# Layer 3 of a four-layer convolution and attention kernel: ScalarE copies the second head pair's scores, VectorE masks the copies in place

## The chip, the cores and the metric

The kernel runs on one core of a Trainium2 chip. The metric is the device time of one execution in microseconds (us). Before the change three runs took 3665.39, 3681.4 and 3687.82 us; the median is 3681.4.

## The reference, cut to what matters

The input x is 4 images of 256 channels, 48 by 48, in fp32. Four layers follow each other, each of the form x = x + layer(group norm(x)): a 7x7 dilated attention kernel, two 3x3 convolutions, and, as layer 3, windowed linear attention. Only layer 3 is changed:

```python
q = sigmoid(Wq x); k = sigmoid(Wk x); v = (Wv x) / |v|      # 8 heads of 32 channels
Ik  = _integral(k)                     # running sums over rows and columns
Ikv = _integral(k[f] * v[g])
for w in (1, 2, 4):
    ws = 48 // w                       # window 48, 24 or 12, around each pixel
    attn = q . box(Ikv, ws);  norm = q . box(Ik, ws)
    outs.append(attn / (norm + 1e-6))
out = Wout @ concat(outs) + bout
```

For each pixel and each of three window sizes, a head sums k v over the keys in the window around the pixel, and multiplies by q. Swapping the order gives what the kernel computes: scores q . k of all pairs of a pixel and a key that are near enough, times a 0/1 mask (is the key in the pixel's window?), times v.

## The kernel before, in words

**Layer 3's tiles.** An image has 6 row blocks of 8 rows (`RB`). A block of queries is one row block of one image and one half of the channels (4 heads): 4 x 2 x 6 = 48 blocks (`order`). Keys are cut into tiles (a, c) of 8 rows and 16 columns, 128 keys, one a partition: row block a, column block c of 3. A block rb visits the key tiles up to three row blocks away (`tiles_of`, line 1913), 12, 15 or 18 of them, 720 in all. `HALVES` (line 78) are the half windows 24, 12 and 6, numbered wi = 0 (widest), 1 (middle), 2 (narrow). So there are three kinds of tile:

- near tiles, |a - rb| at most 1 (384 of them): all three windows see them (`many`, line 1831);
- tiles two rows away (192): the widest and the middle window;
- tiles three rows away (144): the widest window alone, and no row of queries sees them whole.

For near tiles and those two rows away the widest window holds a middle part of the columns whole (`rows_whole`, line 1739); that part comes from summed states and one set of matmuls a block (`whole`, line 1878). Only the outer columns are worked out from scores, in one strip of 16 columns (c = 0 or 2) or two of 8 (c = 1) (`strips`, line 1747). The order of tiles takes near tiles and others by turns, c = 1, 0, 2, and what near tiles are left over come last.

**One tile.** The loop at line 2077 hands out the work; the helper `InOrder` (line 135) keeps each engine's instructions in the order in which the program names them, and through it every instruction has line 143 in the profile.

1. TensorE: `scores` (line 1763) is called for two pairs of heads. A pair's scores, `s`, take one tile of two PSUM banks; the pool `ps_s` (line 1490) has two such tiles. So the first pair of the next tile needs the banks of this tile's first pair, and the second the second's. A matmul shows as two records; a tile has eight.
2. `masked` (line 1781) makes the masked scores `sm` in SBUF, in one tile a pair (pool `smp`, line 1488, 6 tiles: three tiles' worth). VectorE multiplies scores in PSUM by a mask in SBUF (`of_banks`, line 1825). In tiles two rows away ScalarE copies the middle part instead, unmasked (`copy`, line 1837).
3. GpSimd then multiplies (loop at line 1861), from SBUF to SBUF: in near tiles it makes the narrow window's part from the middle one's, and two rows away it masks ScalarE's copy in place.
4. TensorE: `sums` (line 1890) multiplies the masked scores by v into three accumulators `acc`, two tiles later (`LAG` = 2, line 83). TensorE's queue so reads: scores of tile n, sums of tile n - 2, scores of tile n + 1. At a window's last tile ScalarE copies the accumulator to `stage`.

In a near tile the middle part has 624 elements a partition (c = 1), 448 (c = 0) or 432 (c = 2) for a pair of heads; the strips have 256 (two times 128 with c = 1). Three rows away there are 560 to 768.

**The order within a tile** is written out by hand at lines 1854 to 1860 (`copy` does something two rows away alone, `middle` in near tiles alone):

```python
first, second = zip(ss, pairs)
copy(*second)
middle(*first)
widest(*first)
copy(*first)
middle(*second)
widest(*second)
```

After each tile `advance` (line 237) lets other jobs place a few instructions each: projections of the next image, key sums (`k_sums`, line 1535: VectorE scans `cs` and differences `pt`, GpSimd sums `pt`), norms (`norms`, line 1577: `nhi`, `nlo` on GpSimd), states of the keys (`state`, line 1672), and the end of a block (`prepare`, line 1927, `finish`, line 1960: `o`, `stage`, `out_ps`). They share the engines' queues with the tiles. SP issues the loads.

Of the kernel before, what the change touches and what calls it, by code (L numbers as in the profile page):

```python
# [146 lines left out]
def conv_preact_kernel(  # L147
# [53 lines left out]
    pe, dve, act, pool, sync = (  # L201
        InOrder(tc, e) for e in (nc.tensor, nc.vector, nc.scalar, nc.gpsimd, nc.sync)
    )
# [249 lines left out]
    with (  # L453
# [479 lines left out]
        def load_row(pool_, tag, a):  # L933

            t = pool_.tile([P, NCT, K0, P], F32, tag=tag, name="wrow")
            sync.dma_start(
                out=t, in_=w1[:, a * K0 : (a + 1) * K0, :].rearrange("(ct p) k o -> p ct k o", p=P)
            )
            return t
# [442 lines left out]
        with tc.tile_pool(name="wst", bufs=1) as wst:  # L1382
            for ct in range(NCT):
                fetch_x(0, ct)
            rows = [load_row(k1p, "k1", 0), load_row(vp, "v", MT), load_row(vp, "v", MT - 1)]
# [43 lines left out]
        with (  # L1429
# [11 lines left out]
            first = ExitStack()  # L1441
# [41 lines left out]
    with (  # L1483
# [243 lines left out]
        def rows_seen(wi, a, rb):  # L1727

            h = HALVES[wi]
            return (  # L1730
                max(0, a * RB - h + 1 - rb * RB),
                min(RB, a * RB + RB + h - rb * RB),
            )

        def cols_seen(wi, c):
            h = HALVES[wi]
            return max(0, c * KC - h + (wi > 0)), min(W, c * KC + KC + h)

        def rows_whole(a, rb):

            return abs(a - rb) * RB + RB <= HALVES[0]
# [5 lines left out]
        def strips(c):  # L1747

            (c0, c1), (f0, f1) = cols_seen(0, c), cols_whole(c)
            return [(p0, p1) for p0, p1 in ((c0, f0), (f1, c1)) if p0 < p1]  # L1750

        class Block:
# [28 lines left out]
            def masked(self, a, c, ss):  # L1781

                rb = self.rb
                all0 = rows_seen(0, a, rb), cols_seen(0, c)
                (r0, r1), (c0, c1) = all0
                wis = [wi for wi in range(NW) if seen(wi, a, rb)]
                full = rows_whole(a, rb)
                pieces = {wi: [cols_seen(wi, c)] for wi in wis}
                if full:
                    pieces[0] = strips(c)  # L1790

                def room():

                    t = smp.tile([P, SM_ROOM], F32, tag="sm", name="sm")
                    at, got = 0, {}
                    for wi in wis:
                        nr = rows_seen(wi, a, rb)[1] - rows_seen(wi, a, rb)[0]
                        for p0, p1 in pieces[wi]:
                            n = 2 * nr * (p1 - p0)
                            got[wi, p0] = t[:, at : at + n].rearrange(  # L1800
                                "p (j r w) -> p j r w", j=2, r=nr
                            )
                            at += n
                    assert at <= SM_ROOM
                    return got

                pairs = [room() for _ in ss]

                def view(tiles, wi, rows, cols):
                    y0, _ = rows_seen(wi, a, rb)  # L1810
                    x0 = next(p0 for p0, p1 in pieces[wi] if p0 <= cols[0] and cols[1] <= p1)
                    return tiles[wi, x0][
                        :, :, rows[0] - y0 : rows[1] - y0, cols[0] - x0 : cols[1] - x0
                    ]

                def times_mask(engine, wi, rows, cols, dst, src):
                    mr = rb * RB + rows[0] - (a * RB - HALVES[wi] + 1)
                    mc = cols[0] - (c * KC - MCOL0[wi])
                    nr, ncol = rows[1] - rows[0], cols[1] - cols[0]
                    m = mask[wi][:, mr : mr + nr, mc : mc + ncol]  # L1820
                    engine.tensor_mul(
                        dst, src, m.unsqueeze(1).to_broadcast([P, 2, nr, ncol])
                    )

                def of_banks(s, tiles, wi, rows, cols):
                    src = s[:, :, rows[0] - r0 : rows[1] - r0, cols[0] - c0 : cols[1] - c0]
                    times_mask(dve, wi, rows, cols, view(tiles, wi, rows, cols), src)

                many = seen(NW - 1, a, rb)

                def middle(s, tiles):
                    if full and many:
                        of_banks(s, tiles, 1, rows_seen(1, a, rb), cols_seen(1, c))

                def copy(s, tiles):
                    if full and not many and 1 in wis:
                        rows, cols = rows_seen(1, a, rb), cols_seen(1, c)
                        act.copy(  # L1840
                            view(tiles, 1, rows, cols),
                            s[:, :, rows[0] - r0 : rows[1] - r0, cols[0] - c0 : cols[1] - c0],
                        )

                def widest(s, tiles):
                    if not full:
                        of_banks(s, tiles, 0, *all0)
                        return
                    for cols in pieces[0]:
                        of_banks(s, tiles, 0, (r0, r1), cols)  # L1850

                first, second = zip(ss, pairs)
                copy(*second)
                middle(*first)
                widest(*first)
                copy(*first)
                middle(*second)
                widest(*second)  # L1860
                for tiles in pairs:

                    wi = NW - 1 if many else 1
                    if wi in wis:
                        rows, cols = rows_seen(wi, a, rb), cols_seen(wi, c)
                        src = view(tiles, 1, rows, cols)
                        times_mask(pool, wi, rows, cols, view(tiles, wi, rows, cols), src)
                return pairs
# [40 lines left out]
        def seen(wi, a, rb):  # L1909
            r0, r1 = rows_seen(wi, a, rb)  # L1910
            return r0 < r1
# [165 lines left out]
        for n in range(len(stream) + LAG):  # L2077
            if n < len(stream):
                i, a, c, at, last = stream[n]
# [6 lines left out]
            if n >= LAG:  # L2086
                i, a, c, at, last = stream[n - LAG]
# [60 lines left out]
```

## Time and profile before

| what | value |
|---|---|
| median of three runs | 3681.4 us |
| the profiled execution | 3665.04 us |
| its span | 3663.2 us |
| granted TensorE clock, mean | 0.952 |
| busy over the span: TensorE, VectorE, ScalarE, GpSimd | 3216.3, 2419.0, 677.5, 1661.6 us |
| first and last product of masked scores on VectorE | begin at 1389.7 and 3631.9 us |
| products of masked scores on VectorE (`sm<-s,masks`) | 2592, 1145.8 us |
| score matmul records (`s<-qs,ks`) | 5760, 870.4 us |
| sums (`acc<-sm,vs`) | 14976, 683.0 us |
| masks on GpSimd (`sm<-sm,masks`) | 1152, 822.9 us |
| ScalarE's copies of scores (`sm<-s`) | 384, 123.4 us |

A line of groups names line, engine, operation, what is written and read, shape (partitions x elements, or rows * columns of the array for TensorE) and count; then the busy time and the mean of one in ns; then the idle time just before, and which instruction ended it. A line of the timeline begins with start and length in us of a row of like instructions that follow closely. A line of waits names who waited for whom: us in total, times, longest. A matmul's end is modelled in the profile, and spans on GpSimd are rough.

### The profile page before, as it was taken

To read this page: it belongs to the slowest core of one execution; us is meant where nothing else is said; L and a number is where in the kernel's file an instruction comes from. 1 tells how busy PE (TensorE), PEld (TensorE's weight loads), DVE (VectorE), ACT (ScalarE), POOL (GpSimd) and SP (SyncE) were. 2 spreads that over 40 slices of the span, in tenths; PEclk is the share of its full clock that TensorE was granted. 3 is DMA by queue.
4 is the path that set the end of the run, shared out by engine and by line. 5 is a ranking of instruction groups with operands and counts; after the bars stand their busy time and mean duration, and the time that the engine had idled before them with its cause. 6 is when DMAs were issued, how large, how long until landed. Compare 5 with 4: busy or idle time off the path is not lost. (4 is left out here: it accounts for less than half of the span.)

```text
span 3663.2 us, 73044 instructions
## 1 busy us (share of the span) xinstructions
PE 3216.3 (88%) x28754; PEld 1942.3 (53%) x28754; DVE 2419.0 (66%) x4987; ACT 677.5 (18%) x1557; POOL 1661.6 (45%) x2548
## 2 busy tenths in 40 slices
PE   3689998998997887887899889899998899999998
PEld 2467686786785664443444444444444444444444
DVE  7976587487484365876756576765577656566664
ACT  0012111111114422222101222211222201111100
POOL 0000120030030034787876786776476777454552
PEclk9789999999998898999999999999999999999999
DMA  7746324324314423344533543344223344211222
GB/s 252 227 139 197 105 94 129 112 85 127 102 65 138 136 72 108 122 141 144 149 103 112 157 122 122 108 126 137 81 96 120 119 128 129 64 32 32 66 62 61
DMA packets 373031, 423.29 MB, mean 116 GB/s; under 512 B 129075, under 2 KB 328531, under 8 KB 371539
## 3 DMA queue, kind: packets, MB, share of 16 engines
q1 hardware_dynamic: 371491, 416.32, 36.9%
q8 instruction: 229, 3.75, 0.4%
q0 software_dynamic: 144, 1.52, 0.2%
q14 instruction: 111, 0.91, 0.1%
q10 hardware_dynamic: 1056, 0.79, 0.1%
HBM read 288.79 MB, written 131.25 MB: 115 GB/s over the span
## 5 line engine op out<-in xcount | busy, mean ns | idle before, releaser
L143 DVE TENSOR_TENSOR sm<-s,masks 128x128 f32<-128x128 f32 (+8 forms) x2592 | 1145.8, 496 | 709.7 <-PE s L143 377.7
L143 POOL TENSOR_TENSOR sm<-sm,masks 128x432 f32<-128x432 f32 (+14 forms) x1152 | 822.9, 728 | 711.3 <-DVE sm L143 512.6
L143 PE MATMUL s<-qs,ks 32*128 32x320 f32 (+3 forms) x5760 | 870.4, 505 | 109.4 <-DVE sm L143 72.5
L143 PE MATMUL acc<-sm,vs 128*32 128x64 f32 (+13 forms) x14976 | 683.0, 308 | 32.2 <-POOL sm L143 32.1
L143 PE MATMUL cv<-vx,wt 128*128 128x288 f32 x2080 | 556.9, 423 | 92.3 <-DVE vx L143 49.5
L143 PEld LDWEIGHTS s<-qs,ks 32*128 32x128 f32 x5760 | 353.1, 188 | 479.8 <-issue 195.8
L143 PEld LDWEIGHTS acc<-sm,vs 128*32 128x32 f32 x14976 | 351.0, 111 | 441.6 <-issue 269.4
L143 PEld LDWEIGHTS cv<-vx,wt 128*128 128x128 f32 x2080 | 400.5, 197 | 212.6 <-issue 55.0
L143 POOL MEMSET v<- 128x16 f32 (+1 forms) x120 | 18.6, 215 | 722.4 <-DVE vx L143 628.3
L143 ACT COPY sm<-s 128x234 f32<-128x234 f32 (+5 forms) x384 | 123.4, 343 | 915.8 <-PE s L143 784.4
L143 PE MATMUL cv<-v,wl 128*128 128x384 f32 x1152 | 224.3, 354 | 22.4 <-DVE x L143 8.6
L143 PEld LDWEIGHTS cv<-v,wl 128*128 128x128 f32 x1152 | 214.6, 195 | 32.2 <-issue 15.2
L143 POOL TENSOR_TENSOR pt<-pt 128x144 f32<-128x144 f32 x336 | 185.3, 552 | 23.4 <-DVE pt L143 0.5
L143 POOL TENSOR_TENSOR v<-l2v,v 128x384 fp32r<-128x384 f32 x96 | 109.0, 1165 | 127.4 <-ACT v L143 118.7
L143 POOL TENSOR_TENSOR nhi<-nhi,nq 128x384 f32<-128x384 f32 x144 | 144.9, 1034 | 0.3
L143 PE MATMUL cv<-pad,wl 128*128 128x384 bf16 x864 | 143.1, 327 | 0.0
L143 PE MATMUL out_ps<-o,wout_sb 128*128 128x384 f32 x288 | 124.2, 514 | 12.3 <-DMA rc<-r_d 7.6
L143 ACT COPY stage<-acc 128x384 f32<-128x384 f32 x144 | 64.0, 489 | 303.7 <-PE acc L143 272.7
L143 PE MATMUL out_ps<-stage,wout_sb 128*128 128x384 f32 x288 | 118.4, 493 | 0.7 <-DVE stage L143 0.7
L143 DVE TENSOR_TENSOR vx<-v 128x868 f32<-128x868 f32 x112 | 115.3, 1055 | 0.5
L143 PEld LDWEIGHTS <-wl 128*128 128x128 bf16 x864 | 83.9, 97 | 59.4 <-issue 0.8
L143 DVE SCALAR_TENSOR_TENSOR x<-cv,alpha,x 128x384 f32<-128x384 f32 x144 | 83.9, 610 | 41.7 <-PE cv L143 41.4
(174 smaller groups left out, 3347.4 us busy)
## 6 DMA issues: line engine op xcount, KB each, us to landing
wt<-wt SPq DMA_DIRECT2D x48, 768.0 KB
kb_d<-pt SPq DMA_DIRECT2D x48, 576.0 KB
rc<-r_d SPq DMA_DIRECT2D x192, 144.0 KB
nhi<-kb_d SPq DMA_DIRECT2D x120, 192.0 KB
nlo<-kb_d SPq DMA_DIRECT2D x88, 192.0 KB
o_d<-stage SPq DMA_DIRECT2D x24, 576.0 KB
o<-o_d SPq DMA_DIRECT2D x24, 576.0 KB
wl<-wl_d SPq DMA_DIRECT2D x16, 768.0 KB
```

The lines of the kernel that those rows point to most:

```text
L143: return lambda *args, **kwargs: self.tc.keep_in_program_order(op(*args, **kwargs))
```

## The change

The three helpers are replaced by three others: `copy` (ScalarE copies a window's part of a pair), `cut` (VectorE masks a window's strips from PSUM, as `of_banks` did), and `again` (VectorE multiplies a part in SBUF by its mask, in place). For each kind of tile the order is now written out. In near tiles ScalarE copies the second pair's middle part; VectorE masks the first pair's strips and middle part and the second pair's strips from PSUM, and then the copy in place. Three rows away ScalarE copies the second pair whole, and VectorE masks the copy in place after the first pair. Two rows away the calls come in the order in which they came before.

```diff
-                def middle(s, tiles):
-                    if full and many:
-                        of_banks(s, tiles, 1, rows_seen(1, a, rb), cols_seen(1, c))
...
+                def copy(s, tiles, wi):
+                    rows, cols = rows_seen(wi, a, rb), cols_seen(wi, c)
+                    act.copy(
+                        view(tiles, wi, rows, cols),
+                        s[:, :, rows[0] - r0 : rows[1] - r0, cols[0] - c0 : cols[1] - c0],
+                    )
+
+                def cut(s, tiles, wi):
+                    for cols in pieces[wi]:
+                        of_banks(s, tiles, wi, rows_seen(wi, a, rb), cols)
+
+                def again(tiles, wi):
+                    rows, cols = rows_seen(wi, a, rb), cols_seen(wi, c)
+                    t = view(tiles, wi, rows, cols)
+                    times_mask(dve, wi, rows, cols, t, t)
...
                 first, second = zip(ss, pairs)
-                copy(*second)
-                middle(*first)
-                widest(*first)
-                copy(*first)
-                middle(*second)
-                widest(*second)
+                if not full:
+                    copy(*second, 0)
+                    cut(*first, 0)
+                    again(second[1], 0)
+                elif many:
+                    copy(*second, 1)
+                    cut(*first, 0)
+                    cut(*first, 1)
+                    cut(*second, 0)
+                    again(second[1], 1)
+                else:
+                    if 1 in wis:
+                        copy(*second, 1)
+                    cut(*first, 0)
+                    if 1 in wis:
+                        copy(*first, 1)
+                    cut(*second, 0)
```

More of the change, by code (lines that the diff above doesn't have):

```diff
@@ L1831, in masked @@
                 many = seen(NW - 1, a, rb)
-                def middle(s, tiles):
-                    if full and many:
-                        of_banks(s, tiles, 1, rows_seen(1, a, rb), cols_seen(1, c))
[L1837 to L1850, printed above, removed]
-                first, second = zip(ss, pairs)
-                copy(*second)
-                middle(*first)
-                widest(*first)
-                copy(*first)
-                middle(*second)
-                widest(*second)
+                def copy(s, tiles, wi):
[4 more added lines that the diff above has]
+                    )
```

## The prediction

> **What bounds it now.** I read, in this order: the page, the groups by shape for 2200 to 3600 us, the waits, the timeline. The tiles of layer 3 run from 1389 to 3640 us; nothing outside can change. There TensorE is busy 2042 of 2251 us, VectorE 1491, GpSimd 1504, ScalarE 401, by the window sums:
>
> ```profile
> core 0: us, PE busy (x) PEld busy (x) DVE busy (x) ACT busy (x) POOL busy (x), PEclk, DMA share, GB/s
> 1389.00:3640.00 2251.00, 2041.83 (x22896) 1016.62 (x22888) 1490.62 (x3180) 400.87 (x1044) 1503.60 (x2243) 0.97 0.36 106
> ```
>
> A busy TensorE isn't a full one. In the timeline of 3313 to 3323.5 us each row of `s` is one tile's eight score records, two pairs of heads:
>
> ```profile
> 3313.20 1.56 PE L143 MATMUL s<-qs,ks 32*128 32x384 f32 x8
> 3314.16 2.94 DVE L143 TENSOR_TENSOR sm<-s,masks 128x624 f32<-128x624 f32 x8 [0.37 <-PE s L143]
> ...
> 3315.59 1.94 PE L143 MATMUL s<-qs,ks 32*128 32x384 f32 x8
> 3316.58 0.33 PEld L143 LDWEIGHTS s<-qs,ks 32*128 32x128 f32 x4 [0.70 <-PE s L143]
> ...
> 3317.61 0.74 ACT L143 COPY sm<-s 128x312 f32<-128x312 f32 x2 [1.38 <-POOL sm L143]
> 3318.06 0.49 DVE L143 TENSOR_TENSOR sm<-s,masks 128x128 f32<-128x128 f32 x2 [0.96 <-ACT sm L143]
> ...
> 3321.12 0.91 PE L143 MATMUL s<-qs,ks 32*128 32x320 f32 x8
> ```
>
> Both pairs together take 0.91 us; where the second pair must wait until VectorE has left its banks they take 1.56 to 1.94, and count as busy. Sorting the score records by tile: a group takes 0.77 us (320 columns) or 0.88 (384) undisturbed. The excess over this, with the idle time before it, is 136 us behind near tiles with c=1 and a far tile next, 76 behind c=2, 23 behind c=0, 32 between near tiles, 64 behind tiles three rows away, 50 behind two: 381 us. That is the stake: the two score buffers make TensorE and VectorE take turns. The waits show only a part:
>
> ```profile
> PE s L143 <- DVE sm L143: 72.5, 205, 2.7
> PE acc L143 <- POOL sm L143: 32.1, 39, 5.2
> ```
>
> **The skill.** The Trainium skill, PSUM — Partial Sum Buffer, "PSUM bank collisions raise a hardware error": two engines must not be in one bank at once. So strips of the second pair follow ScalarE's copy: ACT ends at 3318.35 in the rows above for both copies, the second pair's at 3318.03, and DVE starts at 3318.06. SBUF — State Buffer, "Who interferes with whom": a VectorE instruction with two SBUF inputs and a GpSimd one that reads SBUF exclude each other, and the first keeps the port to its end. The trace agrees; VectorE's `stage` product has both inputs in SBUF:
>
> ```profile
> 2519.25 0.55 DVE L143 TENSOR_TENSOR stage<-stage,rc 128x384 f32<-128x384 f32 x1
> 2519.45 1.32 POOL L143 TENSOR_TENSOR sm<-sm,masks 128x216 f32<-128x216 f32 x2 [1.42 <-ACT sm L143]
> ...
> 2522.45 0.78 POOL L143 TENSOR_TENSOR sm<-sm,masks 128x324 f32<-128x324 f32 x1 [0.33 <-DVE sm L143]
> 2522.69 0.96 DVE L143 TENSOR_TENSOR stage<-stage,rc 128x384 f32<-128x384 f32 x1
> ```
>
> Ahead of GpSimd it takes 0.55 us. Behind it, it waits until GpSimd ends (2523.23) and then takes 0.42 more: its own time less 0.14. The products of today read `s` from PSUM and don't meet this.
>
> **The change, part by part.** Durations (means of the groups by shape):
>
> ```profile
> L143 DVE TENSOR_TENSOR sm<-s,masks 128x256 f32<-128x256 f32 x505 | 208.5, 416 | 94.5 <-POOL sm L143 34.7 <-issue 23.8 <-ACT sm L143 16.4
> L143 DVE TENSOR_TENSOR sm<-s,masks 128x624 f32<-128x624 f32 x170 | 136.2, 801 | 101.4 <-PE s L143 85.7 <-POOL sm L143 10.0 <-POOL nhi L143 2.3
> L143 DVE TENSOR_TENSOR sm<-s,masks 128x448 f32<-128x448 f32 x168 | 104.0, 619 | 80.5 <-PE s L143 34.9 <-issue 25.5 <-POOL sm L143 8.8
> L143 POOL TENSOR_TENSOR sm<-sm,masks 128x324 f32<-128x324 f32 x52 | 42.8, 834 | 6.1 <-DVE sm L143 5.9
> L143 ACT COPY sm<-s 128x312 f32<-128x312 f32 x42 | 16.3, 421 | 187.8 <-PE s L143 175.0 <-DVE pt L143 4.0 <-POOL pt L143 4.0
> ```
>
> (1) Removed: 384 middle products from PSUM and 144 whole ones. Added: as many in place, equally long alone: 384 elements with both inputs in SBUF took 0.55 us above, as the line through 0.416 (256) and 0.619 (448) from PSUM gives (0.551). So nothing, as long as GpSimd is out of the way; (4) prices it where it isn't.
>
> (2) Added: 528 ScalarE copies. From 168 elements (298 ns) to 312 (421), 0.85 ns an element over 0.155: 0.54 us for 448, 0.69 for 624, 0.52 for 432, 0.70 to 0.81 for 640 to 768; 384 × 0.58 + 144 × 0.75 = 331 us on an engine busy 401 of 2251. The second pair's scores are there about 0.1 us after VectorE begins a tile (median), so a copy ends at 0.75 to 0.95, before VectorE has done the first pair (0.95 to 1.2): free, except behind `stage`, `state` and sigmoid work on ScalarE's queue. Without that cover it would cost up to its length. I put 15 us, range 0 to 60.
>
> (3) The second pair's banks come free earlier. Near c=1: after two strips, the middle and two strips: 0.48 + 0.72 + 0.40 = 1.60 us, not 2.31; c=0: 1.38, not 1.82; c=2: 1.36, not 1.78. Three rows away: after a copy, about 1.0 to 1.3 us, not 1.5 to 1.8.
>
> (4) The in-place product meets GpSimd. GpSimd starts the first pair's narrow mask 0.15 us after the first middle: 1.35 to 2.2 in c=1. The in-place product, issued at 1.52, waits until 2.2 and takes 0.66: end 2.84 against 2.31. Likewise c=0 2.4 against 1.82, c=2 2.25 against 1.78: about +0.53 × 384 = 203 us of VectorE time, bounded by 0 (GpSimd idle) and +0.95 (behind a 1 us GpSimd job). Three rows away: +0.12 × 144 = 17. VectorE becomes 1491 + 220 = 1711. Behind it on VectorE's queue stand the next tile's first strips: late by that where its scores are already there. Against today's pace that is seldom: VectorE's gap to the next tile is under 0.55 us behind 123 of 384 near tiles, shortfall 34 us in all.
>
> (5) Walking the two queues. Rules from the trace: VectorE has scores 0.91 us (320) or 1.02 (384) after their matmul starts; a release reaches TensorE in 0.15; a second pair alone takes 0.74 or 0.85; sums take 1.25, 1.1, 1.0 us (near c=1, 0, 2), 0.84 to 0.7 (three rows), 0.7 to 0.6 (two). Before, near c=1 starting at 0: scores of the far tile at 1.35 and, second pair, 2.46; sums from 3.31 to 4.06; VectorE ends the far tile at 4.42; next near tile's scores at 4.06 and 4.57, VectorE at 4.97. After: 1.4 and 1.85, sums 2.3 to 3.05, but VectorE is held until 2.76 and releases the far tile's first pair at 3.72; next near scores at 3.87, VectorE at 4.78. Over three pairs (c=1, 0, 2) VectorE starts again after 13.85 before and 13.07 after with tiles three rows away; after 14.4 and 13.1 with tiles two rows away, which ScalarE already copies. There are 48 and 64 such triples, and 48 near tiles without partner (nothing): −(48 × 0.78 + 64 × 1.3) = −121 us. With each block's other work spread evenly (TensorE 0.83, VectorE 0.48 us a tile) a triple still gains 0.7.
>
> (6) What is late next: the second pair's narrow mask on GpSimd waits for the in-place product and ends about 1 us later. `acc` needs it two tiles on: the median slack is over 2.3 us, but moving all near tiles by 1.0 makes 44 late, 36 us.
>
> (7) No DMA, weight load or buffer is added; loads issued by SP keep their places. Two rows away the calls and their order are as before.
>
> Sum: −121 + 36 + 15 = −70. The profiled execution, 3665 us (span 3663), becomes 3595. It lies at the bottom of the runs shown; their median is 16 higher, so I forecast 3611.
>
> **Rivals.** *Given back (0.22).* GpSimd is 86% busy at 1550 to 1850 us; a near tile and one two rows away give it four masks (mean 728 ns on the page, 2.9 us), and its other jobs are (1504 − 823)/720 tiles, 1.9 us for two: 4.8 of the 6.2 us that two tiles take now. If it becomes the bound through the first half, half of −121 goes: −60 + 36 + 15 = −9, 3672. Against: it is half idle after 3200. *The port lock paces VectorE (0.28), slower.* If the in-place product of near tiles takes over 1.5 us on average, not about 1.2, a triple is back at 13.9 to 14.2 and the gain of (5) is gone; then 36 + 15 remain, and a tenth of VectorE's other 344 us, now in the way, 34: +85, 3766. For: GpSimd is busy two thirds of the time, with jobs of 1 us. Against: it decides only from 1.5 us. *The turns vanish wholly (inside the 0.50 of faster):* two thirds of 271 us (the 381 less the idle before scores and the two-row tiles) kept: about −130 net, 3550. That the second pair's banks aren't freed earlier is hardly possible: nothing reads them after the strips.
>
> **Numbers.** Faster 0.50 (likeliest, 3611; its own range 3535 to 3645), within 1% 0.22, slower 0.28; a measurement of this kernel can tell about 1% from no change. The range 3535 to 3750 leaves out the ends of both.
>
> **What would show it.** ScalarE near 730 us in these windows, VectorE near 1710; the mean in-place product of near tiles 1.05 to 1.3 us; score groups behind near c=1 tiles under 1.2 us, not 1.8; `acc` behind GpSimd some 35 us longer. It is wrong if the in-place product averages over 1.5 us, if strips wait for ScalarE in most near tiles, or if `acc` waits for GpSimd grow past 100 us.

## The result, and the profile after

The changed kernel takes 3716.3 us (median of 4 runs, 3715.5 to 3718.5) against 3679.5 us before (median of 4): ratio 1.0105, 95% interval 1.0073 to 1.0137. It is slower by about 37 us; 3611 was forecast. Its profiled execution has a span of 3713.7 us, 50 longer; layer 3's tiles take 2296 us, before 2250. In the lines below PE is TensorE, DVE VectorE, ACT ScalarE and POOL GpSimd.

The window sums, by image: first two together, third, fourth. Columns: stretch, its length, busy time (and instructions) of TensorE, of its weight loads, VectorE, ScalarE, GpSimd, then the granted clock, and share and GB/s of DMA. Before:

```profile
1388.00:2588.00 1200.00, 1066.80 (x11588) 525.86 (x11587) 808.73 (x1693) 231.67 (x589) 884.14 (x1304) 0.95 0.42 126
2588.00:3151.00 563.00, 515.79 (x5773) 257.24 (x5772) 374.60 (x810) 112.69 (x282) 375.86 (x566) 0.98 0.37 111
3151.00:3640.00 489.00, 460.25 (x5538) 234.07 (x5537) 307.86 (x680) 56.72 (x174) 243.61 (x373) 0.99 0.18 52
```

After:

```profile
1393.00:2648.00 1255.00, 1031.38 (x11592) 517.25 (x11596) 873.17 (x1693) 382.09 (x853) 960.35 (x1304) 0.93 0.40 120
2648.00:3226.00 578.00, 496.31 (x5776) 251.40 (x5771) 404.93 (x810) 188.32 (x414) 411.69 (x566) 0.96 0.36 109
3226.00:3690.00 464.00, 416.09 (x5538) 218.90 (x5537) 343.92 (x680) 136.80 (x306) 256.95 (x373) 0.99 0.18 53
```

This is the first thing to see: the change loses 55 and 15 us in the first three images and gains 25 in the fourth. Before the fourth, other jobs (projections of the next image, key sums, norms) share the queues. VectorE has 131 us more in all, ScalarE 306 more, and GpSimd 125 more, though GpSimd got no work.

What was to come out did come out: the score groups hardly take turns any more. Groups of the page, before (the first line) and after:

```profile
L143 PE MATMUL s<-qs,ks 32*128 32x320 f32 (+3 forms) x5760 | 870.4, 505 | 109.4 <-DVE sm L143 72.5
```

```profile
L143 PE MATMUL s<-qs,ks 32*128 32x320 f32 (+3 forms) x5760 | 727.2, 508 | 171.3 <-DVE sm L143 90.4
L143 DVE TENSOR_TENSOR sm<-sm,masks 128x624 f32<-128x624 f32 (+2 forms) x528 | 532.2, 1008 | 1.3 <-ACT sm L143 0.3
```

Busy time on scores falls from 870.4 to 727.2 us, at almost the same mean length of one: more of them overlap. The idle time before them grows from 109.4 to 171.3. The timeline of one c=1 tile of the fourth image:

```profile
3369.16 1.60 DVE L143 TENSOR_TENSOR sm<-s,masks 128x128 f32<-128x128 f32 x5 [0.97 <-POOL sm L143]
3369.27 0.68 ACT L143 COPY sm<-s 128x624 f32<-128x624 f32 x1 [1.18 <-PE s L143]
...
3370.51 1.31 PE L143 MATMUL s<-qs,ks 32*128 32x384 f32 x8 [0.41 <-DVE sm L143]
3370.53 0.69 POOL L143 TENSOR_TENSOR sm<-sm,masks 128x270 f32<-128x270 f32 x1 [1.46 <-DVE sm L143]
3370.68 1.21 DVE L143 TENSOR_TENSOR sm<-sm,masks 128x624 f32<-128x624 f32 x1
```

VectorE is through with both pairs' banks after 1.60 us, as worked out, and the next tile's scores take 1.31 us; that is also the median behind all 128 tiles with c=1, where it was 1.94 before. The in-place product is issued 0.15 us after GpSimd's mask and ends at 3371.89: 0.67 after GpSimd ends at 3371.22. This is the wait for the port of step (4), and the rule: of the 128 such products, 122 began while GpSimd was at work, and they end 0.66 us after its instruction (median).

The lock also works the other way, and this the prediction didn't price. In layer 3, 236 of GpSimd's operations began inside an in-place product of VectorE. A step of the key sums (`pt<-pt`) took 0.92 us there (47 of them) and 0.57 elsewhere (289), a product of the norms (`nhi<-nhi,nq`) 1.51 us (25) and 1.03 elsewhere (119). Against the means of like operations outside, the 236 took 96 us more in all: most of GpSimd's 125, though its spans are rough.

Where the time went instead, in the waits of TensorE. Before:

```profile
PE s L143 <- DVE sm L143: 72.5, 205, 2.7
PE acc L143 <- POOL sm L143: 32.1, 39, 5.2
PE s L143 <- ACT sm L143: 27.8, 71, 3.8
PE proj_ps L143 <- ACT sg L143: 17.2, 18, 2.4
PE proj_ps L143 <- ACT vt L143: 11.6, 11, 1.9
PE norm_ps L143 <- POOL nhi L143: 4.7, 3, 3.1
```

After:

```profile
PE s L143 <- DVE sm L143: 90.4, 152, 3.7
PE acc L143 <- POOL sm L143: 80.3, 69, 5.6
PE s L143 <- ACT sm L143: 72.9, 145, 4.0
PE proj_ps L143 <- ACT sg L143: 30.6, 30, 3.2
PE proj_ps L143 <- ACT vt L143: 16.0, 21, 2.1
PE norm_ps L143 <- POOL nhi L143: 11.6, 5, 6.0
```

Sums waiting for GpSimd rise from 32.1 to 80.3 us, projections waiting for ScalarE from 28.8 to 46.6. The trace's records, sorted by what TensorE did or stood before, give the balance over layer 3: time in score groups 839 to 703 us (−136), idle before scores 109 to 171 (+62), before sums 39 to 89 (+50), before projections 30 to 49 (+20), before norms 7 to 15 (+7), small ones +6. That is +9, and layer 3 grew by 46. The other 37 us are busy time of matmuls that the change didn't touch: sums 720 to 739, norms 56 to 69, projections 172 to 178.

A good part of this is the clock. In layer 3 TensorE stood at half clock for 153 us before (29 stretches) and 228 after (41), and was busy in 135 and 186 of them; in matmuls other than scores, 89 and 134. If half clock doubles a matmul's time, this is worth about 22 of the 37 us, an estimate; the remainder isn't explained. One such place, the timeline after:

```profile
1818.23 3.72 POOL L143 TENSOR_TENSOR nhi<-nhi,nlo 128x384 f32<-128x384 f32 x3
...
1821.92 2.17 POOL L143 TENSOR_TENSOR pt<-pt 128x144 f32<-128x144 f32 x4
...
1824.42 2.89 POOL L143 TENSOR_TENSOR nhi<-nhi,nq 128x384 f32<-128x384 f32 x3
...
1825.46 3.39 PE L143 MATMUL norm_ps<-nhi,head_sel 128*32 128x384 f32 x6 [6.01 <-POOL nhi L143]
...
1827.27 1.26 POOL L143 TENSOR_TENSOR sm<-sm,masks 128x252 f32<-128x252 f32 x2
```

and the window sums there:

```profile
1822.40:1829.00 6.60, 3.54 (x10) 0.76 (x14) 0.00 (x0) 0.00 (x0) 5.83 (x9) 0.50 0.63 189
```

GpSimd is busy from 1818 to 1828. Three norm differences take 3.72 us beside an in-place product (3.22 in the same place before), and the masks of a tile that VectorE finished at 1817 come at 1827. GpSimd was late already: it began these differences 0.3 us before TensorE's preceding norm matmuls (1818.50), in the same place before 2.9 us ahead of them. TensorE, whose queue is in order, stands 6.01 us at a norm; before, the same matmul waited 3.05:

```profile
1799.71 2.75 PE L143 MATMUL norm_ps<-nhi,head_sel 128*32 128x384 f32 x5 [3.05 <-POOL nhi L143]
```

The Trainium skill, TensorE: Matmul & The Clock Gate, "Part 1: The HAM clock gate (the "warmup" mystery)", says that TensorE falls back to half clock after an idle window of about 3.4 us and is released after about 3.4 us of sustained work. The stretches here last 3.4 us or small multiples of it, and this one (6.8 us from 1822.3) begins in the gap. Others came without such a gap (last section), so an idle window of that length was not behind each of them. No run changed the clock alone, so its share is read and not isolated.

### The profile page after: what moved, and what is told of

The parts are those of the page before. It is cut to its first block, busy times and chain, and to the rows that moved or that the text cites. A ratio compares the mean times of both kernels' runs of the same rounds, so it can differ in the third digit from the quotient of the medians.

```text
span 3713.7 us, 73668 instructions
## 1 busy us (share of the span) xinstructions
PE 3120.2 (84%) x28754; PEld 1915.3 (52%) x28754; DVE 2549.7 (69%) x4987; ACT 983.7 (26%) x2085; POOL 1786.9 (48%) x2548
## 5 line engine op out<-in xcount | busy, mean ns | idle before, releaser
L143 DVE TENSOR_TENSOR sm<-s,masks 128x128 f32<-128x128 f32 (+6 forms) x2064 | 806.5, 440 | 609.0 <-PE s L143 495.2
L143 POOL TENSOR_TENSOR sm<-sm,masks 128x432 f32<-128x432 f32 (+14 forms) x1152 | 879.9, 780 | 636.1 <-DVE sm L143 506.8
L143 PE MATMUL s<-qs,ks 32*128 32x320 f32 (+3 forms) x5760 | 727.2, 508 | 171.3 <-DVE sm L143 90.4
L143 ACT COPY sm<-s 128x624 f32<-128x624 f32 (+4 forms) x912 | 450.5, 496 | 1548.1 <-PE s L143 1371.4
L143 PE MATMUL acc<-sm,vs 128*32 128x64 f32 (+13 forms) x14976 | 701.1, 310 | 81.0 <-POOL sm L143 80.3
L143 PEld LDWEIGHTS s<-qs,ks 32*128 32x128 f32 x5760 | 314.5, 189 | 444.6 <-issue 197.7
L143 DVE TENSOR_TENSOR sm<-sm,masks 128x624 f32<-128x624 f32 (+2 forms) x528 | 532.2, 1008 | 1.3 <-ACT sm L143 0.3
L143 POOL TENSOR_TENSOR pt<-pt 128x144 f32<-128x144 f32 x336 | 207.2, 617 | 22.9
L143 POOL TENSOR_TENSOR nhi<-nhi,nq 128x384 f32<-128x384 f32 x144 | 156.5, 1113 | 0.3
L143 POOL TENSOR_TENSOR nhi<-nhi,nlo 128x384 f32<-128x384 f32 (+3 forms) x112 | 113.6, 1037 | 0.2
```

What stands on the lines that cost most here:

```text
L143: return lambda *args, **kwargs: self.tc.keep_in_program_order(op(*args, **kwargs))
```

## The experiments

Three theories were put to the test: *port* (the in-place product and GpSimd keep each other off SBUF, and late GpSimd work stops TensorE), *ScalarE* (copies and waits on its queue), *order* (GpSimd merely starts later). Each kernel is measured against the kernel before on the same chip.

**The new order alone.** No ScalarE copies and no in-place products; tiles three rows away keep the old calls. In near tiles:

```diff
-                    copy(*second, 1)
                     cut(*first, 0)
                     cut(*first, 1)
                     cut(*second, 0)
-                    again(second[1], 1)
+                    cut(*second, 1)
```

> Near tiles alone: the new order (strips of the first pair, its middle, strips of the second, its middle), all of it still from PSUM, no copy by ScalarE; tiles three rows away as before. Port theory (the loss comes from the in-place product and GpSimd keeping each other off SBUF): within 8 us of before. ScalarE theory (the loss comes from the copies on ScalarE's queue): within 8 us too. Order theory (the loss comes from GpSimd's masks simply starting later): 20 to 40 us slower, with the wait of acc for GpSimd above 50 us.

3679.8 us against 3661.1: ratio 1.0044 (1.0026 to 1.0061), 16 us by the ratio. TensorE's waits stay as before (sums for GpSimd 31.9 us, idle time in layer 3 208 us, before 207); what grew is its busy time, by 16 us, with 177 us of it at half clock, before 135. Order is no more than a part, and not by way of late masks.

**The order, and copies that nobody needs.** `copy(*second, 1)` comes first again, and `cut(*second, 1)` writes over it.

> As order_only, and ScalarE copies the second pair's middle part as in the change, but VectorE then writes over it from PSUM, so no product has two inputs in SBUF and the banks come free no earlier. ScalarE theory: 20 to 45 us slower than order_only, projections waiting longer for ScalarE. Port theory: at most 10 us slower than order_only.

3708.4 us, 1.0128 (1.0093 to 1.0163): about 30 us over the new order alone, though the two intervals allow 12 to 50. By the records, scores wait 12 us longer, their groups take 7 more, and projections wait 8 longer than in order_only. So copies that add 203 us of busy time to a ScalarE that is idle three quarters of layer 3 are not free. But this kernel has a cost that the changed one doesn't have: VectorE writes over the copy from the same banks, and its masks wait 100.6 us for ScalarE's copies, in order_only 66.0 and in the changed kernel 17.7. How much of the 30 us is ScalarE's queue and how much this wait isn't shown, so for the changed kernel 30 us is not the price of the copies.

**The change in near tiles alone.**

```diff
                 if not full:
-                    copy(*second, 0)
                     cut(*first, 0)
-                    again(second[1], 0)
+                    cut(*second, 0)
```

> The change in near tiles alone, tiles three rows away as before. All theories: most of the loss, 20 to 50 us slower than before. Port theory: the acc wait for GpSimd as in the changed kernel (about 80 us on TensorE, before 32).

3709.5 us, 1.0127 (1.0095 to 1.0158): the whole loss. Idle before sums is 66 us by the records (before 39, changed kernel 89), and half-clock stretches in layer 3 number 41 (before 29).

**Near tiles, without the in-place product.** As in the change in near tiles alone, but `again(second[1], 1)` is left out, so the second pair's middle part stays unmasked.

> As near_only, with the in-place product of near tiles left out (the second pair's middle part stays unmasked, which leaves out part of the computation). Port theory: the score banks' gain of 50 to 100 us comes out, so 40 to 120 us faster than before. ScalarE theory: within 20 us of before or slower, since all copies remain.

3595.8 us, 0.9815 (0.9778 to 0.9852): 65 us faster, with all copies of near tiles in place. So the in-place product costs 114 us. But it takes VectorE's work away as well as the port.

**The same work on VectorE without the port.** The second pair's middle part stays unmasked; VectorE sums it instead:

```diff
-                    times_mask(dve, wi, rows, cols, t, t)
+                    rows2, cols2 = rows_seen(NW - 1, a, rb), cols_seen(NW - 1, c)
+                    dve.tensor_reduce(
+                        view(tiles, NW - 1, rows2, cols2)[:, :, 0, 0],
+                        t.rearrange("p j r w -> p j (r w)"),
+                        AX.X,
+                        ALU.add,
+                    )
```

> As near_only, but in place of the in-place product VectorE sums the same copied elements (one SBUF input, so nothing shared with GpSimd by the skill), and the second narrow mask on GpSimd waits for it in the same way; the second pair's middle part stays unmasked. Port theory: the loss goes, 10 to 60 us faster than before, with the sums at about 0.15 us plus 1.04 ns an element (0.6 to 0.8 us), masks on GpSimd as short as before. Theory that VectorE's added work and GpSimd's longer wait alone cost it: still 20 to 50 us slower, as near_only.

3622.4 us against 3672.2: 0.9862 (0.984 to 0.9885), 50 us faster. The sum reads the same elements at the same place in the queue, and GpSimd's second mask waits for it alike. The second SBUF input (the mask) is gone; it also writes two sums instead of a product for each element, but alone the two are equally long (624 elements with GpSimd idle: 0.80 us and 0.79, from 5 and 6 instances). The groups by shape of near_only and of this kernel:

```profile
L143 DVE TENSOR_TENSOR sm<-sm,masks 128x624 f32<-128x624 f32 x128 | 153.4, 1199 | 0.0
L143 DVE TENSOR_TENSOR sm<-sm,masks 128x432 f32<-128x432 f32 x128 | 118.9, 929 | 0.0
L143 DVE TENSOR_TENSOR sm<-sm,masks 128x448 f32<-128x448 f32 x128 | 116.4, 910 | 0.0
```

```profile
L143 DVE TENSOR_REDUCE sm<-sm 128x2 f32<-128x624 f32 x128 | 101.4, 793 | 0.0
L143 DVE TENSOR_REDUCE sm<-sm 128x2 f32<-128x448 f32 x128 | 78.1, 610 | 0.0
L143 DVE TENSOR_REDUCE sm<-sm 128x2 f32<-128x432 f32 x128 | 76.0, 593 | 0.0
```

0.30 to 0.41 us each, 133 us of VectorE; and GpSimd's busy time in layer 3 is 1513 us here, 1578 in near_only, 1504 before. GpSimd's operations that began inside VectorE's product took 54 us more than like ones outside in near_only (152 of them); those that began inside a sum took no more here (145). Ratio 1.0127 against 0.9862 is a swing of about 97 us for the port, both sides of it together. In the two profiles layer 3 differs by 93 us: TensorE's idle time falls by 55 (before scores 159 to 121, before sums 66 to 52), its busy time by 39, and what of that is at half clock from 212 to 134. This decides for the port theory as the main cause of the loss in near tiles.

**The change three rows away alone.** Near tiles keep the old order.

> The change in tiles three rows away alone. If the two parts add up, the difference of the changed kernel and near_only: 0 to 10 us slower than before. Port theory: within 10 us of before, since few masks of GpSimd run there.

3722.3 us, 1.0133 (1.0113 to 1.0154): 49 us slower, against all expectation, since near_only has the whole loss too. The parts don't add. In its profiled execution layer 3 itself is 41 us longer; the other 16 lie ahead of layer 3, where the kernel is unchanged. The waits of the profile here have the line

```profile
DVE sm L143 <- ACT sm L143: 102.2, 156, 1.3
```

(56.6 before, 17.7 in the changed kernel). With old near tiles in front the second pair's scores come late; copy (0.7 us) and in-place product (0.82 to 1.07) then follow each other where one product of 0.73 to 0.94 stood. Behind new near tiles the scores are early and the copy is covered. This is read from the profile; no run takes it apart further.

**The fourth image alone.** Both new branches get `and self.b == B - 1`; the other images keep the old calls.

> The whole change for the fourth image alone, where no projections, key sums and norms for a next image share the queues; the other three as before. Theory that the other jobs' queues turn the change into a loss: 15 to 28 us faster than before (the changed kernel's fourth image took 463 us, before 487). If the loss were the change's own: no gain, or up to 15 us slower.

3642.4 us, 0.9916 (0.9894 to 0.9937): 30 us faster. It beats both kernels. The in-place products are no shorter in this image (624 elements: 1.25 us), so VectorE's wait for the port alone doesn't turn the gain into a loss.

**Without GpSimd's norm work,** in the kernel before and in the changed one; the norms then lack these differences and products:

```diff
-                for wi, h in enumerate(HALVES):
-                    n = min(RB, max(0, h + 1 - rb * RB))
-                    if n < RB:
-                        pool.tensor_sub(hi[:, wi, n:RB], hi[:, wi, n:RB], lo[:, wi, n:RB])
                 yield 1
-                for wi in range(NW):
-                    pool.tensor_mul(hi[:, wi], hi[:, wi], qf)
```

> The kernel before with GpSimd's differences and products for the norms left out (nhi minus nlo, times nq: about 248 us of GpSimd's time in layer 3; the norms lack them). By itself this should bring at most some 40 us, since GpSimd isn't what paces the kernel before.

3607.5 us, 0.9824 (0.9788 to 0.986): 62 us faster, more than expected. GpSimd did hold up the kernel before.

> The changed kernel with the same norm work of GpSimd left out. Theory that GpSimd's load from other jobs, made longer by the port, turns the change into a loss: now 10 to 40 us faster than lite_before. Theory that ScalarE's queue (projections waiting) does it: 20 to 45 us slower than lite_before, as without the cut.

3596.6 us, 0.9793 (0.9762 to 0.9823): the change is now 11 us faster than lite_before rather than 37 slower, as the theory of GpSimd's load says, though the intervals of the two overlap. What is clear is that 48 us came back, from 37 slower to 11 faster. VectorE's wait for the port is no shorter here (in-place products of 624 elements 1.24 us, 1.20 in the changed kernel), so it is GpSimd's load, its late norms included, that turned the sign. TensorE's waits for the changed kernel without this work:

```profile
PE s L143 <- DVE sm L143: 89.1, 150, 3.7
PE s L143 <- ACT sm L143: 73.2, 146, 2.8
PE proj_ps L143 <- ACT sg L143: 31.1, 30, 2.7
PE acc L143 <- POOL sm L143: 25.0, 43, 2.9
```

and one for the kernel before without it:

```profile
PE acc L143 <- POOL sm L143: 7.2, 12, 2.5
```

Sums wait 25.0 us for GpSimd, not 80.3; the waits for ScalarE stay. So they cost something, and don't decide the sign.

## Why the prediction was wrong

The step that failed is (4), and (5) and (6) behind it: the port's lock was charged to VectorE alone, and GpSimd was taken to keep its pace. In its own terms the sum was −121 + 36 + 15 = −70. Measured in the profile are −74 for the scores (−136 of groups, +62 of idle time), +50 before sums, +20 before projections, +13 before norms and the rest, and +37 of busy time in other matmuls: +46. Step by step:

- (1) and (3) hold, and nothing in the runs speaks against (7). An in-place product that finds GpSimd idle takes 0.79 us for 624 elements, as from PSUM; the second pair's banks come free as worked out.
- (2) ScalarE was put at 15 us, range to 60. The copies took 327 us (331 worked out). Projections wait 20 us longer, within the range; "free, except behind other work" looked at the copies, and left out what queues behind them, the sigmoid and v copies for which TensorE waits. The 30 us of order_act have another wait in them and don't price this.
- (4) The port was seen, and VectorE's part of it priced too high: in-place products of near tiles took 1.03 us on average, not about 1.2, and VectorE gained 131 us, not 220. What failed is that the step charged VectorE alone, though the prediction itself says that the two exclude each other. GpSimd's side, +125 us on the engine that was 74% busy in the first two images, stood nowhere in the sum. reduce_same, without the lock, is 50 us faster than the kernel before; lite_after, with less work for GpSimd and VectorE's wait as it was, is 11 us faster than lite_before.
- (5) is the largest miss by size: −121 us, −30 an image. In the fourth image it is right: −25 in the profile, −30 in last_image. Over all images scores gave −74. The walk followed TensorE and VectorE with other work spread evenly, and let GpSimd and the other jobs follow. What the lock takes of this shows in near tiles: counted in the same way, scores give −37 in near_only and −89 in reduce_same.
- (6) The wait of sums for late masks was put at 36 us, by moving all masks by 1.0 us against today's slack, as if GpSimd had time. Measured: +50.
- At nothing stood the longer busy time of other matmuls, +37, of which the clock is an estimated 22, and the +13 before norms and others.

None of the three signs of being wrong that the prediction named came: in-place products stayed under 1.5 us, VectorE's masks waited for ScalarE only 28 times, and sums waited 80.3 us for GpSimd, not over 100. They watched VectorE and the sums; the loss was spread over several smaller terms.

The rival *given back* named the place (GpSimd in the first half) and stopped at zero. The rival *the port lock paces VectorE* named the sign and the port, but its test, an in-place product over 1.5 us, did not come true: the mean is 1.03. Its size for VectorE was not what decided; the lock made GpSimd late as well.

What stays open: how the loss divides between late masks, late norms and the clock, which come together in the same places (lite_after takes away the norms' work and their waits in one); and why the two parts of the change, each about as slow as the whole, don't add beyond what far_only's waits show.

## What to carry to other kernels

Before moving a product from PSUM to SBUF, look at what GpSimd does at that moment: with two inputs in SBUF the product and GpSimd take turns, and both engines must be charged. When a step makes an engine late, walk every in-order queue that waits for it, with the jobs of other stages in it, since one late norm stops all matmuls behind it. A change that pays in one stage and costs in another can be kept for the first alone: the fourth image by itself gave 30 us.

## What the runs showed of the hardware

- Sums along the free axis of 624 elements in SBUF took 0.793 us beside a busy GpSimd, a product with two SBUF inputs of the same size 1.20, a product from PSUM 0.80.
- GpSimd pays for the shared port too: its `nhi<-nhi,nq` products took 1.51 us when they began inside an in-place product of VectorE and 1.03 otherwise (changed kernel); inside VectorE's sums they took 1.01 us, otherwise 1.04 (reduce_same).
- The wait for the port is inside VectorE's recorded time: the product issued at 3370.68 shows 1.21 us, of which 0.54 is waiting for GpSimd.
- TensorE's clock fell to half for 3.4 us or more not only behind gaps of several us: the trace of before has a stretch of 6.8 us at 2493.0 us, with TensorE busy 83% of the 4 us ahead of it and no gap over 0.51 us.
